# A channel mix on one Trainium2 core: two 64-row contractions in place of one block-diagonal contraction over 128 rows

## The chip, the cores and the metric

The kernel runs on one core of a Trainium2 chip. The metric is the device time of one execution in microseconds. Three runs of the kernel before gave 2972.39, 2974.68 and 2974.85 us; the median is 2974.68 us.

## The reference, cut to what matters

An input of 4 images with 64 channels of 256 x 256 goes through four layers. Layers 0, 1 and 3 are long convolutions: each channel is convolved causally with a separable 256 x 256 filter that a small network generates, and the input times a bias is added. Layer 2 is the one that the change touches. It takes a 2-D Haar transform of every channel, scales the coefficients, mixes the 64 channels at every coefficient with a 64 x 64 matrix, shrinks the result towards zero, does this with two sets of weights, adds the two, transforms back and adds the input:

```python
f1 = haar2d(x)
acc = jnp.zeros_like(f1[:, :conv_w.shape[1]])
for i in range(v.shape[0]):                       # 2 sets
    f3 = f1 * v[i]
    f4 = jnp.einsum('bchw,oc->bohw', f3, conv_w[i])   # 64 channels -> 64
    f5 = jnp.sign(f4) * jax.nn.relu(jnp.abs(f4) - tau[i])
    acc = acc + f5
y = haar2d(acc, inverse=True)
return y + x
```

The scale v[i] doesn't depend on the channel, so the kernel applies it after the mix.

## The kernel before

The kernel has one function, `conv_seq_kernel`, which writes its instructions in an order that it plans itself. Every piece of work is registered with `at(tick, place, run, unit)`; at the end the pieces are sorted by tick and place and run. A tick holds one step each of several pipelines, so that one image's mixing lies among the convolutions of the next image. The tile framework then adds the semaphores and may exchange neighbours on an engine[...].

For each image b there are three stages.

- `convolutions(b, ...)`: per channel, layers 0 and 1 (`first` and `second` twice, each with one `contract`, four TensorE instructions at L190 and L191), the Haar transform along the width on VectorE (`pairs`, `levels`: L257, L258, L269, L270), a split into two parts (`split`, L280 on ScalarE and L281 on VectorE), and along the height on TensorE (`down`, L288). The coefficients go to memory (`coef`).
- `mixing(b, start, n_act)`: 64 groups g, one per tick. `load` fetches a tile `f` of 128 partitions x 2 x 256: partitions 0 to 63 hold the 64 channels of one block of coefficient rows (k = 0), partitions 64 to 127 those of the other block (k = 1); a group has two rows q of each block. `mix` (L335) multiplies them by the weights on TensorE. The result `px` has the coefficient's column on the partitions and 1024 numbers per partition, two PSUM banks: for each half h of the columns, each row q, each block r, both weight sets i and the 64 outputs o. VectorE scales the first `16 - n_act` of the 16 pieces of 64 (L357), ScalarE the other `n_act` one by one (L359). `n_act` is 12 for images 0 to 2 and 6 for image 3. `shrink` takes the size and the sign on ScalarE (L365, L366) and subtracts the threshold on VectorE (L367); `signed` (L372) and `add` (L376) finish on VectorE. `add` writes into `z`, which holds all mixed coefficients of an image.
- `inverse(b, ...)`: per channel c, ScalarE gathers the channel out of `z` with a strided copy (L396), TensorE transforms along the width (L403, L404) and the height (L416), and VectorE joins the parts (L420, L423, L424). Layer 3 follows, at once or, for a third of the channels, put off to the mixing of the last image (`convolution`).

In `mix`, `wb` is a 128 x 256 matrix. Its upper 64 rows hold the weights of both sets in columns 0 to 127 and zeros in the rest; its lower 64 rows hold zeros and then the same weights. So one instruction with 128 rows and 256 columns does both blocks, and half of the products are with zero:

```python
for q in range(2):
    for h in range(2):
        nc.tensor.matmul(ps[:, h, q, :], f[:, q, h * P : (h + 1) * P],
                         wb.rearrange("p r n -> p (r n)"), start=True, stop=True)
```

`psx` has two buffers of two banks for `px`, `psm` four banks for all other products. Every fp32 product appears in the trace as two passes, each with a load of the stationary operand and a stream of the moving one; so the four instructions of a group are 8 matmul records and 8 load records.

Of the kernel before, what the change touches and what calls it, by code (L numbers as in the profile page):

```python
# [9 lines left out]
F32 = mybir.dt.float32  # L10
# [6 lines left out]
B, C, S, EMB, ORD = 4, 64, 256, 33, 64  # L17
P = 128
# [19 lines left out]
def conv_seq_kernel(ctx, tc, x, fz, fw, bias, decay, haar, haar_row, factors, vt, taut, wmix, out):  # L38
# [14 lines left out]
    nc = tc.nc  # L53

    const = ctx.enter_context(tc.tile_pool(name="const", bufs=1))
# [3 lines left out]
    zpool = ctx.enter_context(tc.tile_pool(name="zpool", bufs=1))  # L59
# [4 lines left out]
    psx = ctx.enter_context(tc.tile_pool(name="psx", bufs=2, space=PSUM))  # L64
# [4 lines left out]
    hbr = const.tile([P, P], F32R, name="hbr")  # L69
    hrow = const.tile([P, 2, P], F32, name="hrow")  # L70
    hsinv, ident = hrow[:, 0, :], hrow[:, 1, :]
    wb = const.tile([P, 2, P], F32, name="wb")
    bsb = const.tile([P, 3, C], F32, name="bsb")


    z = zpool.tile([P, 2, S, C], F32, name="z")

    sd = zpool.tile([P, 8, 2, 2, P], F32, name="sd")
    keep = [dram.tile([C, P, 2, 2, P], F32, name=f"keep{b}") for b in range(B)]
# [4 lines left out]

    room = z.rearrange("p h r c -> p (h r c)")
    free = [0]

    def part(n, parts=P):  # L90
        free[0] += n
        return room[:parts, free[0] - n : free[0]]
# [55 lines left out]
    def constants():  # L148
        signs = part(P)
        nc.sync.dma_start(hbt, haar[0])  # L150
        nc.sync.dma_start(signs, haar[1])
        nc.sync.dma_start(hrow, haar_row)
        nc.vector.memset(wb, 0.0)
        for r in range(2):
            nc.sync.dma_start(wb[r * C : (r + 1) * C, r, :], wmix)
        nc.scalar.copy(hb, signs)
        nc.scalar.copy(hbr, hbt)

# [19 lines left out]
    def toeplitz(layer, c, name):  # L178

        t = tp.tile([P, 2, S], F32, name=name, tag="toep")  # L180
        nc.sync.dma_start(t, ap(pads[layer], c * 2 * ROW, [[1, P], [ROW, 2], [1, S]]))
        return t
# [33 lines left out]

    def butterfly(b):

        d = mx.tile([P, 2, C], F32, name=f"bfly_{b}", tag="mag")
        nc.vector.tensor_sub(d, z[:, :, 0, :], z[:, :, 1, :])  # L220
        nc.vector.tensor_add(z[:, :, 0, :], z[:, :, 0, :], z[:, :, 1, :])
        nc.vector.tensor_copy(z[:, :, 1, :], d)

# [2 lines left out]
    def at(tick, place, run, unit):  # L228
        events.append((tick, place, len(events), run, unit))
# [86 lines left out]
    def mixing(b, start, n_act):  # L316

        st = {}

        def load(g):  # L320
            f = mx.tile([P, 2, S], F32, name=f"f_{b}_{g}", tag="f", bufs=3)
            nc.sync.dma_start(f, coef[b].rearrange("k c p w -> (k c) p w")[:, 2 * g : 2 * g + 2])
            st[g] = {"f": f}
            if g % GT == 0:
                t = mx.tile([P, 2, GT, 16], F32, name=f"vt_{b}_{g}", tag="vt")
                nc.sync.dma_start(t, scales[g // GT])
                st["vt", g // GT] = t

        def scale(g, i):
            return st["vt", g // GT][:, i, g % GT, :]  # L330

        def over(g, i, n):
            return scale(g, i)[:, :n].unsqueeze(2).to_broadcast([P, n, C])

        def mix(g):  # L335
            f = st[g]["f"]
            ps = psx.tile([P, 2, 2, S], F32, name=f"px_{b}_{g}", tag="mix")
            for q in range(2):
                for h in range(2):
                    nc.tensor.matmul(  # L340
                        ps[:, h, q, :],
                        f[:, q, h * P : (h + 1) * P],
                        wb.rearrange("p r n -> p (r n)"),
                        start=True,
                        stop=True,
                    )
            if g == 0:

                one, two = ps[:, :, 0, :P], ps[:, :, 0, P:]
                d = mx.tile([P, 2, P], F32, name=f"d_{b}", tag="mag")  # L350
                nc.vector.tensor_copy(d, two)
                nc.vector.tensor_sub(two, one, d)
                nc.vector.tensor_add(one, one, d)
            f4 = mx.tile([P, 16, C], F32, name=f"f4_{b}_{g}", tag="f4")
            px = ps.rearrange("p h q (r i o) -> p (h q r i) o", r=2, i=2)
            n = 16 - n_act
            nc.vector.tensor_tensor(f4[:, :n], px[:, :n], over(g, 0, n), ALU.mult)  # L357
            for j in range(n, 16):
                nc.scalar.mul(f4[:, j], px[:, j], scale(g, 0)[:, j : j + 1])  # L359
            st[g]["f4"] = f4  # L360

        def shrink(g):
            f4 = st[g]["f4"]
            mag = mx.tile([P, 16, C], F32, name=f"mag_{b}_{g}", tag="mag")
            nc.scalar.activation(mag, f4, AF.Abs)  # L365
            nc.scalar.activation(f4, f4, AF.Sign)  # L366
            nc.vector.tensor_sub(mag, mag, over(g, 1, 16))  # L367
            st[g]["mag"] = mag

        def signed(g):  # L370
            mag = st[g]["mag"]
            nc.vector.scalar_tensor_tensor(mag, mag, 0.0, st[g]["f4"], ALU.max, ALU.mult)  # L372

        def add(g):
            parts = st.pop(g)["mag"].rearrange("p (h r i) o -> p h r i o", h=2, i=2)
            nc.vector.tensor_add(z[:, :, 4 * g : 4 * g + 4, :], parts[:, :, :, 0, :], parts[:, :, :, 1, :])  # L376

        for g in range(S // 4):
            at(start + g - 2, 0, load, g)

            for s, (place, stage) in enumerate([(-2.5, mix), (-3.5, shrink), (-4.1, signed), (-4.2, add)]):
                at(start + g + s, place, stage, g)

    def inverse(b, start, put_off):

        st = {}

        def fetch(c):  # L390
            if c == 0:
                butterfly(b)
            r = mx.tile([P, 2, 2, P], F32, name=f"r_{b}_{c}", tag="f", bufs=3)
            nc.sync.dma_start(r, keep[b][c])
            a = mx.tile([P, 2, 2, P], F32, name=f"zc_{b}_{c}", tag="mag")
            nc.scalar.copy(a, z[:, :, :, c].rearrange("p h (i k) -> p h k i", k=2))  # L396
            st[c] = {"r": r, "z": a}

        def rows(c):
            a = st[c]["z"]  # L400
            ps = psm.tile([P, 2, 2, P], F32, name=f"pw_{b}_{c}", tag="mm")
            for m in range(2):
                nc.tensor.matmul(ps[:, m, 0, :], a[:, 0, m, :], hsinv, start=True, stop=True)  # L403
                nc.tensor.transpose(ps[:, m, 1, :], a[:, 1, m, :], ident)  # L404
            w = mx.tile([P, 2, 2, 2, P], F32R, name=f"w_{b}_{c}", tag="f4")
            nc.scalar.copy(w[:, 0], ps)  # L406
            nc.vector.tensor_tensor(w[:, 1], ps, w[:, 0].bitcast(F32), ALU.subtract)
            st[c]["w"] = w
            if c not in put_off:
                st[c][2] = toeplitz(2, c, f"t2_{b}_{c}")  # L410

        def cols(c):
            ps = psm.tile([P, 2, 2, P], F32, name=f"pu_{b}_{c}", tag="mm")
            flat = "p m e w -> p (m e w)"
            for i in range(2):
                nc.tensor.matmul(  # L416
                    ps.rearrange(flat), hb, st[c]["w"][:, i].rearrange(flat), start=(i == 0), stop=(i == 1)
                )
            t = io.tile([P, 2, 2, P], F32, name=f"t_{b}_{c}", tag="res", bufs=BUFS["res"])
            nc.vector.scalar_tensor_tensor(t, st[c]["r"], 0.5, ps, ALU.mult, ALU.add)  # L420
            u = io.tile([P, 2, S], F32, name=f"u_{b}_{c}", tag="y", bufs=BUFS["y"])
            v = u.rearrange("p m (w e) -> p m w e", e=2)
            nc.vector.tensor_add(v[:, :, :, 0], t[:, :, 0, :], t[:, :, 1, :])  # L423
            nc.vector.tensor_sub(v[:, :, :, 1], t[:, :, 0, :], t[:, :, 1, :])  # L424
            st[c]["u"] = u

        ends = last(b, st)
        for c in range(C):

            at(start + c, -1, fetch, c)  # L430
            at(start + c + 1, -9, rows, c)
            at(start + c + 2, -8, cols, c)
            if c in put_off:
                at(start + c + 3, -5, lambda c: nc.scalar.dma_start(late[b, c], st.pop(c)["u"]), c)
            else:
                for s, stage in enumerate(ends):
                    at(start + c + 3 + s, s - 7, stage, c)
# [28 lines left out]
    one, two, three = filters(0, nc.scalar), filters(1, nc.scalar), filters(2, nc.sync)  # L466
# [12 lines left out]
    for tick, do in enumerate([constants, None, None, *three[:-1], *tables()], 4):  # L479
        if do is not None:  # L480
            at(tick, 3, lambda unit, do=do: do(), 0)
# [4 lines left out]
    start = ready + 3  # L486
    for b in range(B):
# [10 lines left out]
        start = max(end + C, ready + 3)  # L498
# [112 lines left out]
```

## Time and profile before

The profiled execution took 2975.2 us and its span is 2973.4 us, so 1.8 us lie around the span; it stands 0.5 us above the median of the runs.

| | busy us | share of the span |
|---|---|---|
| PE (TensorE matmul) | 2913.8 | 98% |
| PEld (TensorE loads of the stationary operand) | 2615.1 | 88% |
| DVE (VectorE) | 2545.5 | 86% |
| ACT (ScalarE) | 2156.9 | 73% |
| L340 PE, the mix | 488.2 | 2048 records, mean 380 ns |
| L340 PEld, its loads | 369.5 | 2048 records, mean 190 ns |

A row of the groups reads: line, engine, operation, output<-inputs, shapes, number, then busy time, mean of one in ns, and the idle time just before with what ended it. Matmuls are pipelined: [...] neighbours overlap, and the spacing of the starts tells how fast they follow each other. In the timeline, "x8" means that eight instructions of a kind were merged into one row. The granted clock is full in all slices.

Mixing of image 0 lies at about 453 to 845 us, of image 1 at 1110 to 1515, of image 2 at 1780 to 2185 and of image 3 at 2440 to 2708. L340 is found nowhere else.

### The profile page before, as it was taken

To read this page: it belongs to the slowest core of one execution; us is meant where nothing else is said; L and a number is where in the kernel's file an instruction comes from. 1 tells how busy PE (TensorE), PEld (TensorE's weight loads), DVE (VectorE), ACT (ScalarE), POOL (GpSimd) and SP (SyncE) were. 2 spreads that over 40 slices of the span, in tenths; PEclk is the share of its full clock that TensorE was granted. 3 is DMA by queue.
4 is the path that set the end of the run, shared out by engine and by line. 5 is a ranking of instruction groups with operands and counts; after the bars stand their busy time and mean duration, and the time that the engine had idled before them with its cause. 6 is when DMAs were issued, how large, how long until landed. Compare 5 with 4: busy or idle time off the path is not lost. (4 is left out here: it accounts for less than half of the span.)

```text
span 2973.4 us, 52066 instructions
## 1 busy us (share of the span) xinstructions
PE 2913.8 (98%) x16950; PEld 2615.1 (88%) x16950; DVE 2545.5 (86%) x4571; ACT 2156.9 (73%) x5014; POOL 0.2 (0%) x4
## 2 busy tenths in 40 slices
PE   8999999999999999999999999999999999999999
PEld 6898988888888898888888988888888988888998
DVE  5766768999998879999989879999998889998776
ACT  2333338999986758889986668989986768887554
POOL 0000000000000000000000000000000000000000
PEclk9999999999999999999999999999999999999999
DMA  5877777666667876776777876777777878777676
GB/s 159 247 237 226 229 228 212 203 202 207 207 196 244 250 217 200 208 216 204 208 219 244 250 225 197 209 210 211 207 216 237 256 236 235 233 230 217 212 212 186
DMA packets 562497, 649.73 MB, mean 219 GB/s; under 512 B 44369, under 2 KB 447412, under 8 KB 562100
## 3 DMA queue, kind: packets, MB, share of 16 engines
q1 hardware_dynamic: 482996, 562.07, 64.8%
q10 hardware_dynamic: 79232, 84.34, 8.0%
q8 instruction: 137, 2.24, 0.3%
q14 instruction: 132, 1.08, 0.1%
HBM read 426.77 MB, written 219.48 MB: 217 GB/s over the span
## 5 line engine op out<-in xcount | busy, mean ns | idle before, releaser
L190 PE MATMUL py<-t,a 128*128 128x256 f32 x3072 | 919.0, 381 | 8.9 <-ACT a L199 5.5
L199 ACT COPY a<-pa 128x512 f32<-128x512 f32 x768 | 477.2, 621 | 387.9 <-PE pa L191 357.2
L359 ACT ACTIVATE f<-px,vt 128x64 f32<-128x64 f32 x2688 | 582.3, 358 | 143.5 <-DVE f L357 143.4
L191 PEld LDWEIGHTS py<-t,a 128*128 128x128 f32 x3072 | 583.4, 190 | 79.3
L191 PE MATMUL py<-t,a 128*128 128x128 f32 x3072 | 590.0, 274 | 0.0
L190 PEld LDWEIGHTS py<-t,a 128*128 128x128 f32 x3072 | 500.4, 191 | 50.9 <-ACT a L199 12.4
L340 PE MATMUL px<-wb,f 128*128 128x256 f32 x2048 | 488.2, 380 | 4.9 <-ACT f L359 4.9
L340 PEld LDWEIGHTS px<-wb,f 128*128 128x128 f32 x2048 | 369.5, 190 | 47.0 <-ACT f L359 6.7
L367 DVE TENSOR_TENSOR mag<-mag,vt 128x1024 f32<-128x1024 f32 x256 | 312.4, 1220 | 28.3 <-ACT mag L365 26.9
L190 PE MATMUL pa<-t,y 128*128 128x256 f32 x1024 | 311.6, 386 | 22.4 <-DVE y L212 20.3
L406 ACT CAST w<-pw 128x512 fp32r<-128x512 f32 x256 | 150.2, 587 | 227.0 <-PE pw L404 218.9
L372 DVE SCALAR_TENSOR_TENSOR mag<-mag,f 128x1024 f32<-128x1024 f32 x256 | 311.7, 1218 | 1.9
L190 PE MATMUL pa<-t,x 128*128 128x256 f32 x1024 | 305.9, 380 | 0.4 <-issue 0.4
L365 ACT ACTIVATE mag<-f 128x1024 f32<-128x1024 f32 x256 | 293.7, 1147 | 11.0 <-DVE z L376 8.8
L366 ACT ACTIVATE f<-f 128x1024 f32<-128x1024 f32 x256 | 285.2, 1114 | 3.0
L396 ACT COPY zc<-z 128x512 f32<-128x512 f32 x256 | 282.0, 1103 | 0.7 <-ACT w L406 0.4
L281 DVE TENSOR_TENSOR sp<-sd,sp 128x512 fp32r<-128x512 f32 x256 | 176.1, 688 | 91.4 <-ACT sp L280 90.2
L190 PE MATMUL pa<-t,u 128*128 128x256 f32 x772 | 232.8, 383 | 2.9 <-PE pu L416 1.6
L420 DVE SCALAR_TENSOR_TENSOR t<-r,pu 128x512 f32<-128x512 f32 x256 | 174.9, 683 | 60.4 <-PE pu L416 57.0
L212 DVE SCALAR_TENSOR_TENSOR y<-x,bsb,py 128x512 f32<-128x512 f32 x256 | 190.1, 742 | 37.9 <-PE py L191 36.1
L212 DVE SCALAR_TENSOR_TENSOR y<-y,bsb,py 128x512 f32<-128x512 f32 x256 | 190.0, 742 | 34.2 <-PE py L191 33.1
L191 PEld LDWEIGHTS pa<-t,x 128*128 128x128 f32 x1024 | 194.6, 190 | 26.3
(67 smaller groups left out, 4458.9 us busy)
## 6 DMA issues: line engine op xcount, KB each, us to landing
t<-pad SPq DMA_DIRECT2D x768, 256.0 KB, 3.9
x<-in_x SPq DMA_DIRECT2D x256, 256.0 KB, 3.6
keep<-sd SPq DMA_DIRECT2D x256, 256.0 KB, 2.9
coef<-co SPq DMA_DIRECT2D x256, 256.0 KB, 3.3
f<-coef SPq DMA_DIRECT2D x256, 256.0 KB, 3.2
r<-keep SPq DMA_DIRECT2D x256, 256.0 KB, 3.3
out_y<-y ACTq DMA_DIRECT2D x256, 256.0 KB, 3.6
late<-u ACTq DMA_DIRECT2D x63, 256.0 KB, 2.9
```

Of the source, the lines that this page charges most:

```text
L190: nc.tensor.matmul(ps[:, m, :], src[:, 0, m * P : (m + 1) * P], t[:, ::-1], start=True, stop=False)
L191: nc.tensor.matmul(ps[:, m, P:], src[:, 1, m * P : (m + 1) * P], t[:, : P - 1 : -1], start=False, stop=True)
L199: nc.scalar.copy(a, ps)
L212: nc.vector.scalar_tensor_tensor(y, s[res], bsb[:, layer, c : c + 1], ps, ALU.mult, ALU.add)
L281: nc.vector.tensor_tensor(w[:, 1], t, w[:, 0].bitcast(F32), ALU.subtract)
L340: nc.tensor.matmul(ps[:, h, q, :], f[:, q, h * P : (h + 1) * P], wb.rearrange("p r n -> p (r n)"), start=True, stop=True,)
L359: nc.scalar.mul(f4[:, j], px[:, j], scale(g, 0)[:, j : j + 1])
L365: nc.scalar.activation(mag, f4, AF.Abs)
L366: nc.scalar.activation(f4, f4, AF.Sign)
L367: nc.vector.tensor_sub(mag, mag, over(g, 1, 16))
L372: nc.vector.scalar_tensor_tensor(mag, mag, 0.0, st[g]["f4"], ALU.max, ALU.mult)
L396: nc.scalar.copy(a, z[:, :, :, c].rearrange("p h (i k) -> p h k i", k=2))
```

## The change

`wb` becomes a 128 x 128 matrix: the same weights of both sets, once in the upper and once in the lower 64 rows, with no zeros; the memset of the zeros goes. `mix` contracts each block's 64 channels by themselves: 8 instructions of 64 rows and 128 columns in place of 4 of 128 rows and 256 columns. The block r = 0 uses partitions 0 to 63, r = 1 uses 64 to 127, in turn. In the built program each of the 8 carries a tile of 64 x 128 of the array, at row 0 for r = 0 and at row 64 for r = 1; all other matmuls, save the two first products of a filter's network with 33 rows each, carry 128 x 128. All of block 0's results lie in one PSUM bank and all of block 1's in the other.

The order of the 16 pieces in `px` follows: block, half, row, set instead of half, row, block, set. So `z` gets the block as an outer dimension, `add`, `butterfly`, the gather at L396 and the tables that the host lays out (`coefficients`, `factors`) change their indices. The number of instructions, the elements of each and the transfers stay as they are. In the built programs TensorE's list is the same but for 8 rows in place of 4 per group; on the other engines' lists some neighbours change places.

```diff
-    wb = const.tile([P, 2, P], F32, name="wb")
+    wb = const.tile([P, P], F32, name="wb")
...
-    z = zpool.tile([P, 2, S, C], F32, name="z")
+    z = zpool.tile([P, 2, 2, P, C], F32, name="z")
...
-        nc.vector.memset(wb, 0.0)
         for r in range(2):
-            nc.sync.dma_start(wb[r * C : (r + 1) * C, r, :], wmix)
+            nc.sync.dma_start(wb[r * C : (r + 1) * C], wmix)
...
-            ps = psx.tile([P, 2, 2, S], F32, name=f"px_{b}_{g}", tag="mix")
-            for q in range(2):
-                for h in range(2):
-                    nc.tensor.matmul(
-                        ps[:, h, q, :],
-                        f[:, q, h * P : (h + 1) * P],
-                        wb.rearrange("p r n -> p (r n)"),
-                        start=True,
-                        stop=True,
-                    )
+            ps = psx.tile([P, 2, 2, 2, P], F32, name=f"px_{b}_{g}", tag="mix")
+            for h in range(2):
+                for q in range(2):
+                    for r in range(2):
+                        rows = slice(r * C, (r + 1) * C)
+                        nc.tensor.matmul(
+                            ps[:, r, h, q, :], f[rows, q, h * P : (h + 1) * P], wb[rows], start=True, stop=True
+                        )
...
-            px = ps.rearrange("p h q (r i o) -> p (h q r i) o", r=2, i=2)
+            px = ps.rearrange("p r h q (i o) -> p (r h q i) o", i=2)
...
-            parts = st.pop(g)["mag"].rearrange("p (h r i) o -> p h r i o", h=2, i=2)
-            nc.vector.tensor_add(z[:, :, 4 * g : 4 * g + 4, :], parts[:, :, :, 0, :], parts[:, :, :, 1, :])
+            parts = st.pop(g)["mag"].rearrange("p (s q i) o -> p s q i o", q=2, i=2)
+            rows = z.rearrange("p r h i c -> p (r h) i c")[:, :, 2 * g : 2 * g + 2, :]
+            nc.vector.tensor_add(rows, parts[:, :, :, 0, :], parts[:, :, :, 1, :])
...
-            nc.scalar.copy(a, z[:, :, :, c].rearrange("p h (i k) -> p h k i", k=2))
+            nc.scalar.copy(a, z[:, :, :, :, c].rearrange("p k h i -> p h k i"))
```

More of the change, by code (lines that the diff above doesn't have):

```diff
@@ L83, in conv_seq_kernel @@
     late = dram.tile([B, C, P, 2, S], F32, name="late")
-    room = z.rearrange("p h r c -> p (h r c)")
+    room = z.rearrange("p r h i c -> p (r h i c)")
     free = [0]
@@ L217, in butterfly @@
     def butterfly(b):
+        one, two = z[:, 0, :, 0, :], z[:, 1, :, 0, :]
         d = mx.tile([P, 2, C], F32, name=f"bfly_{b}", tag="mag")
-        nc.vector.tensor_sub(d, z[:, :, 0, :], z[:, :, 1, :])
-        nc.vector.tensor_add(z[:, :, 0, :], z[:, :, 0, :], z[:, :, 1, :])
-        nc.vector.tensor_copy(z[:, :, 1, :], d)
+        nc.vector.tensor_sub(d, one, two)
+        nc.vector.tensor_add(one, one, two)
+        nc.vector.tensor_copy(two, d)
     events = []
@@ L336, in mix @@
             f = st[g]["f"]
-            ps = psx.tile([P, 2, 2, S], F32, name=f"px_{b}_{g}", tag="mix")
-            for q in range(2):
-                for h in range(2):
-                    nc.tensor.matmul(
-                        ps[:, h, q, :],
-                        f[:, q, h * P : (h + 1) * P],
-                        wb.rearrange("p r n -> p (r n)"),
-                        start=True,
-                        stop=True,
-                    )
+            ps = psx.tile([P, 2, 2, 2, P], F32, name=f"px_{b}_{g}", tag="mix")
[6 more added lines that the diff above has]
+                        )
             if g == 0:
-                one, two = ps[:, :, 0, :P], ps[:, :, 0, P:]
+                one, two = ps[:, 0, :, 0, :], ps[:, 1, :, 0, :]
                 d = mx.tile([P, 2, P], F32, name=f"d_{b}", tag="mag")
@@ L570, in coefficients @@
         a = a.reshape(2, S, S)[:, down][:, :, along]
-        return lay(a.reshape(2, S // 4, 4, 2, P).transpose(4, 1, 3, 2, 0).reshape(P, S // 4, 16))
+        return lay(a.reshape(2, S // 4, 2, 2, 2, P).transpose(5, 1, 3, 4, 2, 0).reshape(P, S // 4, 16))
     local = _haar_local()
@@ L576 @@
     scaled = (half * np.float32(math.sqrt(0.5)))[level]
-    rows = np.repeat(np.abs(local).max(axis=1), 2).reshape(1, S // 4, 1, 4, 1)
+    rows = np.abs(local).max(axis=1).reshape(1, S // 4, 1, 1, 2, 1)
     signs = np.sign(local)
@@ L580 @@
         [
-            (rows**power * np.stack([first, np.full(P, second)], axis=1).reshape(P, 1, 2, 1, 1) * np.ones((1, 2))).reshape(
+            (rows**power * np.stack([first, np.full(P, second)], axis=1).reshape(P, 1, 1, 2, 1, 1) * np.ones((2, 1, 1, 2))).reshape(
                 P, S // 4, 16
```

## Prediction

> **What bounds the kernel now.** I read the share of busy time first, then the four stretches in which L340 runs, then the waits in them, then the timeline of one group. The page's first view:
>
> ```profile
> PE 2913.8 (98%) x16950; PEld 2615.1 (88%) x16950; DVE 2545.5 (86%) x4571; ACT 2156.9 (73%) x5014; POOL 0.2 (0%) x4
> ```
>
> TensorE is the first suspect, but the share is a mean over stages. The busy time by stretch, for the mixing of images 0, 1, 2 and 3 (columns: stretch, its length, then busy us with counts of PE, PEld, DVE, ACT, POOL, then clock, DMA share, GB/s):
>
> ```profile
> 453.00:830.00 377.00, 368.25 (x2020) 325.41 (x2019) 359.10 (x623) 346.71 (x993) 0.00 (x0) 1.00 0.68 205
> 1110.00:1510.00 400.00, 394.74 (x2206) 354.14 (x2205) 375.21 (x657) 355.20 (x1001) 0.00 (x0) 1.00 0.71 207
> 1780.00:2180.00 400.00, 394.82 (x2209) 354.35 (x2208) 372.64 (x652) 356.45 (x1003) 0.00 (x0) 1.00 0.71 207
> 2440.00:2715.00 275.00, 268.24 (x1447) 238.26 (x1445) 269.66 (x314) 238.76 (x569) 0.00 (x0) 1.00 0.79 233
> ```
>
> The reader is to see two things. PE is the bound where the mix runs (99% in the second and third stretch). And VectorE stands close behind: it leaves 17.9, 24.8, 27.4 and 5.3 us, together 75 us. In the last stretch it is busier than PE. Whatever TensorE saves, these stretches can't lose more than about 75 us.
>
> The waits between 1110 and 1510 us say what VectorE's 25 idle us are:
>
> ```profile
> DVE y L212 <- PE py L191: 10.7, 14, 1.2
> DVE mag L367 <- ACT mag L365: 6.8, 9, 1.3
> DVE sp L281 <- ACT sp L280: 2.6, 8, 0.8
> ```
>
> Less than half is waiting for TensorE; the rest waits for ScalarE, which is 89% busy there. The timeline of PE around one group:
>
> ```profile
> 1400.36 1.89 PE L340 MATMUL px<-wb,f 128*128 128x256 f32 x8
> 1402.09 0.38 PE L190 MATMUL py<-t,a 128*128 128x256 f32 x1
> ```
>
> The next work starts 1.73 us after the group's first pass: 8 passes of 0.216 us, with no gap. All 256 groups take 256 x 1.73 = 443 us of TensorE's time. That is what the change bears on.
>
> [...] L112, with 33 rows, and L340, with 128, both have loads of about 0.19 us (183 at the least, 190). So halving the rows makes no load and no pass shorter by itself; all gain must come from two tiles working at once.
>
> **The change part by part.** *Passes.* A group becomes 8 products of 128 columns, so 16 passes and 16 loads. The price of a 128-column pass is in the timeline of L403 and its loads:
>
> ```profile
> 1000.69 0.30 PEld L403 LDWEIGHTS pw<-hrow,zc 128*128 128x128 f32 x2
> 1000.91 0.14 PEld L404 LDWEIGHTS pw<-hrow,zc 128*128 128x128 f32 x1
> ...
> 1000.80 0.39 PE L403 MATMUL pw<-hrow,zc 128*128 128x128 f32 x2
> 1001.02 0.27 PE L404 MATMUL pw<-hrow,zc 128*128 128x128 f32 x1
> ```
>
> Two passes in 0.22 us: one per 0.11 us. Two loads of 0.19 us each end 0.30 us after the first began, so loads too follow each other at 0.11 us. In the 256-column passes of before, the loads had time to spare; with 128 columns load and stream are equally long. Two bounds follow. If the two row halves both load and stream side by side, the 16 passes take 8 x 0.11 = 0.88 us. If only one load can be under way at a time, streams side by side are worth nothing, since a pass needs its load: 16 x 0.11 = 1.76 us. Against 1.73 that is -0.85 or +0.03 us a group. [...] I take the first, and keep the second as the rival.
>
> *Mode switches.* Each group now switches from 128-row to 64-row tiles and back. The listing of the built program has 271 unbroken stretches of L340's successor (241 whole groups, 15 cut in two), so 542 switches. Before has one such switch amid running convolutions, where layer 3's 33-row product (a 64-row tile) comes between two contracts:
>
> ```profile
> 64.14 0.38 PE L191 MATMUL pa<-t,x 128*128 128x128 f32 x2
> 64.46 0.70 PE L112 MATMUL fp<-z 33*128 33x256 f32 x2
> 65.08 0.70 PE L190 MATMUL py<-t,a 128*128 128x256 f32 x2
> 65.62 0.27 PE L191 MATMUL py<-t,a 128*128 128x128 f32 x1
> ```
>
> From 64.14 to 65.62 us is 1.48 us. The passes are 2 of 0.11 and 4 of 0.214, together 1.08. So 0.40 us went into two switches, 0.20 each: the old stream ends, the loads of the new mode start only about 0.1 us later, and the first one isn't hidden. Both products also wait on semaphores, so 0.20 is an upper value if those waits bound; zero is the lower. I take 0.20: the two directions agree[...]. 542 x 0.20 = 108 us.
>
> *Sum on TensorE.* Parallel: 256 x (0.88 - 1.73) + 108 = -218 + 108 = -110 us, some 27 us per stretch. Serial: 256 x 0.03 + 108 = +116 us, 29 per stretch.
>
> *What of it reaches the end.* In the second and third stretch PE is the bound and 27 us would come off, but VectorE's room is 25 and 27 us, and some 10 us of that waits for ScalarE. I take 16 us each. In the first, the PE rows wait for VectorE (L212, 7.4 us) as often as the other way round, and the room is 18: I take 6. In the last, VectorE is 98% busy: 2. Together 40 us. Outside these stretches no L340 runs, and nothing changes.
>
> *Edits with one answer.* L376 writes four runs of 128 in place of two of 256; VectorE's rows for 512 elements take 685 (L376), 688 (L281), 689 (L269, 8-byte steps) and 683 ns (L420) whatever the pattern, so nothing is added or gained. The gather at L396 takes 1103 ns against 621 for L199's copy of as many elements from PSUM; the step in `z` goes from 512 to 256 bytes. It may stay or fall to about 620, 256 x 0.48 = 124 us of ScalarE at most; the inverse stages, where it runs, have ScalarE below 72% and PE at 100%, which hides it. If it grew by as much, ScalarE would stand near 90% there and still not bind. I take nothing. The memset at L153 (0.27 us, at 1.2 us) goes; two small loads of `wb` stay. L357 and L359 read as many elements from two banks as before; ScalarE's wait for L357 stays. No DMA moves past another except neighbours that change places; I take nothing, with 5 us to either side. No wait is added: the group still waits for `f` and a free `px`, and signals once, at its last product.
>
> Against the profiled execution: 2975.2 - 40 = 2935.2 us; the median stands 0.5 below, so **2935 us**.
>
> **The rivals.** *Serial loads (slower).* One mechanism: the load path takes one load at a time whatever the tile, so 16 loads at 0.11 us set the pace, and the switches are pure cost. For it: loads and passes are equally long at 128 columns, and the trace never shows two loads closer than 0.11 us. [...] Price: 29 us in each stretch. First: PE idles 9 us, take 20. Second and third: 28 each. Last: PE idles 7, take 22. Together +98 us: 3073. It decides once a pass of the group comes to over (1.73 - 0.42) / 16 = 0.082 us, between the 0.055 of the parallel and the 0.11 of the serial case.
>
> *Partly parallel.* Streams overlap but the issue of 32 records, or the order first tile twice and then the second, keeps them at 0.07 to 0.10 us a pass: 0.07 gives 256 x (1.12 - 1.73) + 108 = -48 us of PE, of which a third reaches the end, 2960; 0.10 gives +74, about 3035.
>
> *Switches for nothing.* If the 0.20 was the semaphores' and a switch is free, the parallel case saves 54 us a stretch on PE and VectorE becomes the bound everywhere: at most 75 us, 2900. The serial case without it is +8 us, 2980.
>
> **How the numbers follow.** A measurement of this kernel tells some 0.2% (6 us) from no change. Parallel with a switch of 0.20 or less: 0.49 (2900 to 2960, on its own 2935). Serial: 0.38, with switches 0.33 (3045 to 3100), without 0.05. Partly parallel: 0.13 (2955 to 3045), split between the signs. Faster: 0.49 of the first and 0.03 of the last make 0.52, less 0.02 that VectorE takes away: 0.50. Same: 0.07. Slower: 0.43. The range runs from VectorE's bound, 2900, to 3080, which takes in the centre of the serial case; above it lies about 0.15, below it 0.03.
>
> **What would show it.** Right: in the timeline a group of 16 records spans about 0.9 us plus a gap of 0.2 on either side, loads start in pairs closer than 0.11 us, VectorE's share in 1110 to 1510 rises to 97 or 98%, and its waits for L191 shrink. Serial: starts of the mix's matmuls lie 0.11 us apart throughout, and ticks grow by 0.4 us. Wrong in the switches: no gap of 0.2 us at a group's ends. If the gather at L396 or the add at L376 changes by over 0.1 us a piece, my "nothing" for them is wrong.

## The result and the profile after

The changed kernel takes 2993.12 us (median of 4 runs, 2991.24 to 2998.09) against 2974.76 us for the kernel before (4 runs, 2972.39 to 2977.92). The ratio is 1.0064, interval 1.0046 to 1.0081: slower by 18 us, where 40 us less was forecast. The profiled execution took 2998.09 us, its span is 2996.3 us. In the changed file the lines from L190 to L212 stand one lower (L189 is before's L190); L340 became L343, L357 L356, L359 L358, L365 and L367 L364 and L366; L376 and L396 stayed. From the first start of the mix to its last start, the four mixings of before run from 454 to 860, 1092 to 1533, 1766 to 2206 and 2436 to 2708 us, which is wider for images 0 to 2 than was said ahead of the prediction; those of after run from 453 to 864, 1096 to 1540, 1776 to 2222 and 2455 to 2730.

The busy time of the kernel after, on its page:

```profile
PE 2833.4 (95%) x18998; PEld 2512.1 (84%) x18998; DVE 2546.9 (85%) x4570; ACT 2159.9 (72%) x5014; POOL 0.2 (0%) x4
```

TensorE lost 80 us of busy time and the end came 23 us later. The same four stretches as before, each inside a mixing save the last, which begins 15 us ahead of it and ends 15 us short of its end (columns PE, PEld, DVE, ACT, POOL, clock, DMA share, GB/s):

```profile
453.00:830.00 377.00, 345.87 (x2455) 298.99 (x2453) 353.72 (x614) 344.05 (x984) 0.00 (x0) 0.99 0.67 202
1110.00:1510.00 400.00, 374.31 (x2651) 327.79 (x2651) 369.69 (x647) 353.52 (x995) 0.00 (x0) 1.00 0.69 205
1780.00:2180.00 400.00, 371.95 (x2627) 325.72 (x2626) 367.75 (x644) 348.57 (x986) 0.00 (x0) 1.00 0.69 204
2440.00:2715.00 275.00, 246.08 (x1943) 214.40 (x1942) 262.18 (x315) 228.23 (x536) 0.00 (x0) 0.98 0.79 231
```

Every engine is busy for less of the same time than before: in the second stretch PE 20 us, VectorE 5.5 us, ScalarE 1.7 us. So TensorE was relieved and no other engine filled up. And the granted clock, full in every slice of before, is 0.99 and 0.98 in two stretches.

The mix itself did what the prediction expected. The timeline of one group of the kernel after:

```profile
1402.87 0.39 PE L190 MATMUL pa<-t,y 128*128 128x128 f32 x2
...
1403.19 0.97 PEld L343 LDWEIGHTS px<-wb,f 64*128 64x128 f32 x16
1403.19 1.16 PE L343 MATMUL px<-wb,f 64*128 64x128 f32 x16
...
1404.28 0.30 PEld L189 LDWEIGHTS pa<-t,x 128*128 128x128 f32 x2
1404.28 0.70 PE L189 MATMUL pa<-t,x 128*128 128x256 f32 x2
```

The single records behind the x16 (starts in us, from the trace):

```
loads    1403.186 1403.193 | 1403.294 1403.301 | 1403.403 1403.410 | ...
matmuls  1403.188 1403.194 | 1403.401 1403.408 | 1403.513 1403.519 | ... | 1404.071 1404.078
```

The two row tiles start 6 or 7 ns apart, and a pair follows the last by 0.11 us (the second follows the first by 0.21). The last pass of the old mode began at 1402.983, 0.11 us after the one before it, so its stream is put to end at 1403.09; the first stream after the group is put behind its load, at 1404.386, where the next load starts. That is 1.30 us where before had 1.73: 0.43 us less, times 256 groups 110 us. It is no single case: 176 of the 237 groups that stand whole in the trace take, as this one does, 1.296 or 1.297 us from the last start of the old mode to the first recorded start after them.

The waits between 1110 and 1510 us, first of the kernel before (two rows that the prediction didn't show), then of the kernel after (waiting engine and line, what it waited for, us in all, times, longest):

```profile
ACT f L359 <- DVE f L357: 41.1, 42, 2.5
...
PEld pa L190 <- DVE y L212: 8.7, 12, 1.9
```

```profile
ACT f L358 <- DVE f L356: 45.2, 51, 3.4
PEld pa L189 <- DVE y L211: 24.0, 21, 2.1
PE pa L189 <- DVE y L211: 20.0, 20, 2.0
DVE sp L281 <- ACT sp L280: 13.8, 17, 1.1
DVE mag L366 <- ACT mag L364: 10.2, 10, 2.8
```

The first row was there to be read before. ScalarE was busy for 355.2 of those 400 us and waited 41.1 us for VectorE's scaling: 396 us together; for TensorE it waited 2.3 us (L199 <- L191). So it had next to no time that a faster TensorE could fill directly, though its busy share says 89%. VectorE's wait for TensorE (L212 <- L191, 10.7 us) has gone from the top of the list, TensorE's wait for VectorE rose from 8.7 to 24.0 us, and VectorE waits longer for ScalarE (2.6 to 13.8, 6.8 to 10.2).

The granted clock fell to half in four pieces, one in the first mixing and three in the last. Here are the windows just ahead of the four, and then two of the pieces:

```profile
558.90:562.30 3.40, 1.47 (x7) 0.71 (x5) 3.40 (x7) 0.43 (x1) 0.00 (x0) 1.00 0.19 74
2548.90:2552.30 3.40, 1.76 (x21) 1.42 (x19) 3.30 (x5) 3.40 (x9) 0.00 (x0) 1.00 0.91 287
2637.60:2641.00 3.40, 1.25 (x18) 0.97 (x16) 3.40 (x4) 2.99 (x7) 0.00 (x0) 1.00 0.78 233
2716.10:2719.50 3.40, 0.78 (x14) 0.59 (x13) 3.40 (x6) 2.99 (x9) 0.00 (x0) 1.00 0.79 240
```

```profile
562.30:569.13 6.83, 5.76 (x24) 4.86 (x25) 5.54 (x13) 6.43 (x20) 0.00 (x0) 0.50 0.55 151
...
2719.50:2722.91 3.41, 3.41 (x14) 2.77 (x12) 3.12 (x4) 2.44 (x4) 0.00 (x0) 0.50 0.33 117
```

Each piece at 0.50 follows 3.4 us in which PE was busy for 0.78 to 1.76 us, while VectorE was at work nearly throughout. The pieces make 20.5 us at half clock, so up to 10 us of TensorE's work is lost in them, an estimate: half of the 20.5.

### The profile page after: what moved, and what is told of

The parts are those of the page before. It is cut to its first block, busy times and chain, and to the rows that moved or that the text cites. A ratio compares the mean times of both kernels' runs of the same rounds, so it can differ in the third digit from the quotient of the medians.

```text
span 2996.3 us, 56145 instructions
## 1 busy us (share of the span) xinstructions
PE 2833.4 (95%) x18998; PEld 2512.1 (84%) x18998; DVE 2546.9 (85%) x4570; ACT 2159.9 (72%) x5014; POOL 0.2 (0%) x4
## 3 DMA queue, kind: packets, MB, share of 16 engines
q14 instruction: 132, 1.08, 0.1%
## 5 line engine op out<-in xcount | busy, mean ns | idle before, releaser
L189 PE MATMUL py<-t,a 128*128 128x256 f32 x3072 | 945.2, 389 | 48.8 <-ACT a L198 43.0
L358 ACT ACTIVATE f<-px,vt 128x64 f32<-128x64 f32 x2688 | 580.6, 348 | 162.4 <-DVE f L356 162.4
L190 PEld LDWEIGHTS py<-t,a 128*128 128x128 f32 x3072 | 585.2, 190 | 80.2
L190 PE MATMUL py<-t,a 128*128 128x128 f32 x3072 | 591.5, 274 | 0.0
L189 PEld LDWEIGHTS py<-t,a 128*128 128x128 f32 x3072 | 484.5, 191 | 108.1 <-ACT a L198 59.4
L189 PE MATMUL pa<-t,y 128*128 128x256 f32 x1024 | 316.4, 391 | 69.4 <-DVE y L211 69.3
L366 DVE TENSOR_TENSOR mag<-mag,vt 128x1024 f32<-128x1024 f32 x256 | 312.3, 1220 | 30.7 <-ACT mag L364 29.0
L343 PE MATMUL px<-wb,f 64*128 64x128 f32 x4096 | 307.1, 286 | 14.9 <-ACT f L358 14.9
L189 PE MATMUL pa<-t,x 128*128 128x256 f32 x1024 | 308.9, 383 | 1.6 <-issue 1.3
L364 ACT ACTIVATE mag<-f 128x1024 f32<-128x1024 f32 x256 | 292.6, 1143 | 13.6 <-DVE z L376 12.2
L343 PEld LDWEIGHTS px<-wb,f 64*128 64x128 f32 x4096 | 254.8, 188 | 50.6 <-ACT f L358 17.6
L396 ACT COPY zc<-z 128x512 f32<-128x512 f32 x256 | 282.4, 1104 | 9.0 <-DVE z L222 6.2
L365 ACT ACTIVATE f<-f 128x1024 f32<-128x1024 f32 x256 | 283.1, 1106 | 6.3 <-DVE y L211 2.3
L189 PE MATMUL pa<-t,u 128*128 128x256 f32 x772 | 232.8, 383 | 3.6 <-PE pu L416 2.3
L189 PEld LDWEIGHTS pa<-t,y 128*128 128x128 f32 x1024 | 156.4, 192 | 88.7 <-DVE y L211 86.1
L190 PEld LDWEIGHTS pa<-t,y 128*128 128x128 f32 x1024 | 195.1, 191 | 26.6
```

The costliest lines, as they stand in the source:

```text
L189: nc.tensor.matmul(ps[:, m, :], src[:, 0, m * P : (m + 1) * P], t[:, ::-1], start=True, stop=False)
L190: nc.tensor.matmul(ps[:, m, P:], src[:, 1, m * P : (m + 1) * P], t[:, : P - 1 : -1], start=False, stop=True)
L343: nc.tensor.matmul(ps[:, r, h, q, :], f[rows, q, h * P : (h + 1) * P], wb[rows], start=True, stop=True)
L396: nc.scalar.copy(a, z[:, :, :, :, c].rearrange("p k h i -> p h k i"))
```

## The experiments

Three causes were to be told apart: (a) the framework's new order of the instructions; (b) TensorE's saving is real, but the loop between ScalarE and VectorE sets the pace; (c) idling costs TensorE clock. "Mixing lengths" are the time from the first to the last matmul of the mix, in the profiled execution, for images 0 to 3. They are 406.5, 440.5, 440.3 and 271.3 us before and 411.1, 444.0, 445.7 and 275.4 after, so 17.5 of the 23 us lie in them.

**The order and the mix, each alone.** The two programs issue the same pieces, but the framework sorts them a little differently: 865 of 4570 places of VectorE's list, 388 of 5337 of ScalarE's, 145 of 10267 of TensorE's and 91 of 2194 of SP's hold another instruction (so TensorE's list isn't quite the same, as was said ahead of the prediction). Manual dependencies that set no semaphore hold one kernel's order in the other; in the traces the sequence of operations and tiles on VectorE and ScalarE is then the same in every place:

```diff
+    for engine, packed in lists.items():
...
+        for a, b in zip(order, order[1:]):
+            tc.add_manual_dep(own[b], own[a].name,
+                mybir.DependencyInfo(mybir.DependencyClass.NoSync, mybir.DependencyReason.DATA), reason="hold")
+    hold(ORDER)
```

The changed mix with before's order:

> The changed kernel, with the order of instructions on every engine held to that of the kernel before (its mix's 4 products stand as 8). Theory A (order): the framework's scheduler, given the new mix, exchanged neighbours on VectorE, ScalarE and the transfer queue, and those exchanges cost what was lost; with the old order the loss of 18 us goes and some of TensorE's saving shows: 2935 to 2970 us. Theory B (the other engines bound): VectorE and ScalarE pace the mixing whatever their exact order, and the row-tiled mix itself loses the 18 us: 2985 to 3000 us.

The old mix with after's order:

> The kernel before, with the order of instructions on every engine held to that of the changed kernel; the mix is the old block-diagonal one. Theory A (order): the new order is the worse one, so it is slower than before by about 18 us or more, since TensorE here has no saving to set against it: 2990 to 3030 us. Theory B: the order matters little, 2970 to 2982 us.

Measured: 2981.87 us for the first (ratio 1.0024, 1.0014 to 1.0033), 2983.92 for the second (1.0033, 1.0021 to 1.0046), 2974.3 before. Both lie between the two forecasts put down for them: neither cause is the whole. The order costs 9.6 us by itself and the changed mix 7.6 us, together 17 of the 18. Nothing of TensorE's 110 us reached the end with the changed mix. The mixing lengths say the same: 405.5, 441.8, 441.9 and 274.7 for the changed mix in the old order, with none of the 28 us per image gone from them. The stretches between the mixings, where no mix runs, grew too: by 5.5 us in the changed kernel, by 3.9 with the old mix in the new order and by 1.9 with the changed mix in the old one, so most of that goes with the order.

**The threshold left out.** If VectorE's work were the bound, 256 pieces of 1.22 us less would show. From here on each program has the order that the framework gives it, save in the two runs that fill TensorE up again.

```diff
             nc.scalar.activation(f4, f4, AF.Sign)
-            nc.vector.tensor_sub(mag, mag, over(g, 1, 16))
```

With the old mix:

> The kernel before without the subtraction of the threshold (L367 on VectorE is left out, so the shrinking is not done; 256 instructions of 1.22 us, 312 us of VectorE's time). TensorE is the bound of the mixing in the kernel before, so both theories expect little: 2950 to 2975 us.

With the changed mix:

> The changed kernel without the subtraction of the threshold (L366 on VectorE is left out, so the shrinking is not done). If TensorE's saving is real (0.33 us a group, some 84 us in all) and is only kept back by VectorE, it shows here against the old mix with the same part left out: 60 to 85 us less than that, about 2880 to 2900 us. If the saving is not real, or ScalarE alone holds it back, the two are within 20 us of each other.

Measured: 2977.1 us (ratio 1.0008, 1.0000 to 1.0017) and 2963.5 us (0.9961, 0.9947 to 0.9974). The stretch 1110 to 1510 us of the old mix without the threshold, and its first wait:

```profile
1110.00:1510.00 400.00, 392.46 (x2188) 351.65 (x2187) 315.97 (x594) 352.37 (x989) 0.00 (x0) 1.00 0.68 204
```

```profile
ACT f L359 <- DVE f L357: 46.0, 37, 2.5
```

VectorE came down from 375 to 316 us and the kernel was no faster. PE was busy for 98% there too, so this run alone doesn't tell TensorE from ScalarE as the bound. ScalarE's busy time and this one wait still make 398 of 400 us. With the changed mix the kernel is 13.6 us shorter than that, in the branch of the forecast for a saving that is not real or that ScalarE alone holds back (within 20 us), though TensorE had 110 us less to do. But the images differ. The mixing lengths are 405.2, 444.9, 447.1 and 265.7 with the old mix and 401.9, 445.0, 445.3 and 249.6 with the changed one. In images 1 and 2 nothing is gained over before with both TensorE and VectorE relieved: there VectorE's busy time was not the second bound, and what stayed is ScalarE and its wait. In image 3 the changed mix is 16 us shorter than the old one, which fills PE there. The stretch 2440 to 2690 us, old mix first:

```profile
2440.00:2690.00 250.00, 247.73 (x1359) 222.07 (x1358) 195.58 (x239) 218.55 (x519) 0.00 (x0) 1.00 0.81 239
```

```profile
2440.00:2690.00 250.00, 238.58 (x1952) 209.67 (x1951) 206.17 (x254) 234.14 (x558) 0.00 (x0) 1.00 0.83 255
```

So in the last image, where VectorE was 98% busy before, its own work did hold the saving back, as the prediction had it.

**The shrinking left out.** Size, sign, threshold and product are replaced by one copy on VectorE.

```diff
-            nc.scalar.activation(mag, f4, AF.Abs)
-            nc.scalar.activation(f4, f4, AF.Sign)
-            nc.vector.tensor_sub(mag, mag, over(g, 1, 16))
...
-            nc.vector.scalar_tensor_tensor(mag, mag, 0.0, st[g]["f4"], ALU.max, ALU.mult)
+            nc.vector.tensor_copy(mag, st[g]["f4"])
```

With the old mix:

> The kernel before with the shrinking left out (no size, no sign, no threshold, no product; VectorE copies the scaled mix in the product's place), which takes 2.2 us of ScalarE's and about 1.8 us of VectorE's time from each group. Its mixing can only be bound by TensorE then. If TensorE was the bound of the mixing already (my prediction's reading), little changes: 2950 to 2975 us. If VectorE and ScalarE set the pace, 20 to 60 us go: 2915 to 2955 us.

With the changed mix:

> The changed kernel with the same shrinking left out. The trace has a group at 1.30 to 1.40 us with its two switches against 1.73; with both other engines out of the way all of it should come off: 256 x 0.33 to 0.43 us, so 70 to 110 us less than the old mix with the same part left out. If instead row tiling costs TensorE something that the records hide, the two lie within 20 us.

Measured: 2942.18 us (ratio 0.9891, 0.9876 to 0.9906) and 2891.09 us (0.972, 0.9707 to 0.9733): the changed mix is 51 us shorter. The stretch 1110 to 1510 us of the two, old mix first:

```profile
1110.00:1510.00 400.00, 400.00 (x2254) 361.74 (x2253) 296.24 (x620) 254.64 (x909) 0.00 (x0) 1.00 0.73 213
```

```profile
1110.00:1510.00 400.00, 387.05 (x2797) 343.93 (x2796) 305.34 (x648) 259.84 (x931) 0.00 (x0) 1.00 0.73 218
```

In this stretch PE has no gap with the old mix, VectorE and ScalarE have 100 us or more of idle time each, and the saving appears: the mixing lengths fall from 401.1, 430.9, 430.8 and 262.9 to 396.1, 417.7, 420.7 and 242.5. This is the direct evidence that TensorE does get quicker. It is less than half of the 110 us, and short of the 70 to 110 that were expected. PE is at 97% with the changed mix, ScalarE waits 116.5 us for VectorE's scaling there, and 10 us ran at half clock; how the rest is split over these was not settled.

**Two tiles for the results.** ScalarE's wait for L357 was put down to both engines reading one tile. Here each bank is a tile of its own (r = 0 and 1 in the changed mix, the column halves in the old), and ScalarE begins with the pieces of the bank that VectorE doesn't read (8 in images 0 to 2):

```diff
-            ps = psx.tile([P, 2, 2, 2, P], F32, name=f"px_{b}_{g}", tag="mix")
+            ps = [psx.tile([P, 2, 2, P], F32, name=f"px{r}_{b}_{g}", tag=f"mix{r}") for r in range(2)]
...
-            for j in range(n, 16):
-                nc.scalar.mul(f4[:, j], px[:, j], scale(g, 0)[:, j : j + 1])
+            for j in [*range(max(n, 8), 16), *range(n, 8)]:
+                nc.scalar.mul(f4[:, j], px[j // 8][:, j % 8], scale(g, 0)[:, j : j + 1])
```

With the changed mix:

> The changed kernel with its product in two tiles of one bank each, and ScalarE taking the 8 pieces of the second bank first, so that it no longer waits for VectorE's read of the first bank before its first piece (in the last image VectorE reads 10 pieces, so it needs a second, small instruction there). Theory C: ScalarE's wait for VectorE's scaling (48 us of 400 between 1110 and 1510 us in the changed kernel) closes a loop of the two engines, which keeps the pace whatever TensorE does. Without the wait the loop opens and TensorE's saving shows: 2925 to 2965 us. If the pace is set by the sum of VectorE's own work, it stays at 2985 to 3000 us.

With the old mix:

> The kernel before with the same two tiles and the same order of the pieces. Theory C: the loop opens here too, but TensorE stands at 99% in the mixing and takes over at once: 2960 to 2975 us, 10 to 40 us slower than the changed mix with two tiles. If the pace is set by VectorE's own work: 2970 to 2985 us.

Measured: 2974.86 us (ratio 1.0003, 0.9994 to 1.0012) and 2971.1 us (0.9991, 0.9984 to 0.9997). The changed kernel won 18 us by it, the old one 3; the first is above the forecast of an open loop (2925 to 2965), and the changed mix is not yet the faster of the two. Its single runs lie wide apart, from 2966.77 to 2987.6 us. Between 1110 and 1500 us ScalarE's wait for VectorE's scaling fell from 44.4 to 24.2 us with the changed mix and from 39.4 to 1.2 with the old one, where a wait of 30.4 us for TensorE took its place. So the wait came from how the two engines shared the results; whether the one tile made it, or that ScalarE began with pieces of the bank that VectorE reads, was not separated, as the edit changes both. The mixing of images 1 and 2 now is quicker with the changed mix (431.0 and 429.7 against 434.0 and 436.2), but that of image 3 is slower (284.5 against 279.3, both longer than the 271.3 of before): there VectorE has ten pieces, which with two tiles take two instructions. So `n_act` of the last image went from 6 to 8:

```diff
-        mixing(b, start, 12 if b + 1 < B else 6)
+        mixing(b, start, 12 if b + 1 < B else 8)
```

With the changed mix:

> The changed kernel with two tiles, as in the run of two tiles before, and in the last image ScalarE takes 8 pieces in place of 6, so that VectorE reads exactly one bank in one instruction and neither engine waits for the other's bank. In the run before, the last mixing took 284 us against 275 because of VectorE's second instruction (64 of them). Theory C: that comes off again and more, about 20 us: 2945 to 2962 us, faster than both kernels. If ScalarE becomes the bound of the last mixing (2 more pieces of 0.2 us in each of 64 groups, 26 us, on 238 of 275): 2965 to 2980 us.

With the old mix:

> The kernel before with two tiles and 8 pieces for ScalarE in the last image. TensorE, at 99% in the second and third mixing, holds it there; the last mixing gains what the changed one gains, unless TensorE holds that too: 2955 to 2968 us, and 3 to 15 us slower than the changed mix in the same form.

Measured: 2961.97 us (ratio 0.9959, 0.9947 to 0.9972) and 2967.32 us (0.9977, 0.9967 to 0.9987). The first is 12 us shorter than the kernel before and is the best with the whole computation. The changed mix is 5 us better here, but that isn't the mixing's doing alone: in the profiled executions the four mixing lengths together differ by 1.2 us (408.5, 431.9, 431.5 and 270.5 against 405.9, 434.0, 436.4 and 267.4), while 4.1 us lie behind the last mixing, where no mix runs. The orders were not held in these four runs. In the best kernel 1653 of VectorE's 4570 places hold another instruction than in the changed kernel, more than the 865 that cost 9.6 us, so how much of the 18 us, and of the 12, is the order and how much the open loop was not separated. What the traces show is the wait itself. The waits between 1780 and 2180 us, old mix first:

```profile
ACT f L368 <- PE px L340: 30.7, 39, 1.1
...
ACT f L368 <- DVE f L361: 3.8, 8, 1.3
```

```profile
ACT f L366 <- DVE f L359: 28.1, 22, 2.6
PEld pa L189 <- DVE y L211: 23.5, 23, 1.9
...
ACT f L366 <- PE px L343: 2.7, 5, 0.5
```

With two tiles ScalarE waits 30.7 us for the old mix, and 2.7 for the changed one. So the faster mix takes away a wait that now counts, and most of that time becomes a wait for VectorE again. It gains 6.9 us in images 1 and 2, and images 0 and 3, where five of its six pieces at half clock lie, give 5.7 of it back.

**TensorE filled up again.** With before's order held, the changed mix issues the four products of the second half of the columns twice, to the same place:

```diff
-            for h in range(2):
+            for h in (0, 1, 1):
```

> The changed mix with the old order of instructions, and the four products of the second half issued twice, to the same place (the result is the same; 8 more passes a group, 0.44 us, 113 us of TensorE's time in all, about as much as the change saved). The run with the old order but without them took 2981.9 us, 7.6 above before, and had 17 us of half clock in four pieces. If TensorE's time in the mix is worth nothing and the half clock costs the rest: 2974 to 2980 us, with no half clock left. If TensorE's time counts, the 0.44 us show: 3010 us or more. If the rest is the two switches, which stay: about 2982 us.

Measured: 2975.61 us (ratio 1.0006, 1.0000 to 1.0013), beside 1.0024 without the filling: some 113 us more for TensorE (an estimate: 256 groups x 4 pairs of 0.11 us) made the kernel about 6 us faster. No piece runs at half clock any more, in place of 17 us, and the stretch 1110 to 1510 us is before's again:

```profile
1110.00:1510.00 400.00, 394.64 (x3116) 352.10 (x3115) 374.37 (x657) 356.69 (x1008) 0.00 (x0) 1.00 0.70 208
```

```profile
ACT f L358 <- DVE f L356: 41.7, 42, 2.8
```

The mixing of image 3, where the half clock had been, took 270.8 us in place of 274.7; those of images 0 to 2 stayed within 0.7 us. So with one tile TensorE's time in the mix is worth nothing either way, and where it idled more the kernel took 6 us longer. That it is the clock that costs, and not the shifted starts alone, is not shown; it rests on the two going together.

The same filling, for images 0 and 3, in the best kernel, with that kernel's order held:

```diff
-            for h in range(2):
+            for h in (0, 1, 1) if b in (0, B - 1) else (0, 1):
```

> The changed mix in two one-bank tiles, 8 pieces for ScalarE in the last image (2961.97 us), with the order of all instructions held as it was there, and in images 0 and 3 each group's four products of the second half of the columns issued twice, to the same place: 128 x 4 passes in pairs of 0.11 us, some 56 us of TensorE work that nobody needs. Theory (TensorE's saving is not on the path in these stretches, and its idling costs clock): the pieces of 3.41 us at half clock in images 0 and 3 (5 of 6) go, the granted clock is 1.000, and the time stays or falls by up to 8 us: 2954 to 2963. Rival (with the loop between ScalarE and VectorE opened, TensorE's time is on the path again): 56 us more on TensorE bring 10 to 40 us: 2972 to 3002.

Measured: 2980.05 us (ratio 1.001, 1.0003 to 1.0017), 18 us more than without, or 15.5 with each taken against the runs of the kernel before beside it. The theory that was put down for it fell, the rival held. Three pieces of 3.41 us at half clock were left in place of six, and yet the mixing lengths rose from 408.5 to 414.5 in image 0 and from 270.5 to 282.6 in image 3, and stayed in the others (431.8 and 430.2 after 431.9 and 431.5). The stretch 2440 to 2690 us, without and with the filling:

```profile
2440.00:2690.00 250.00, 239.66 (x1801) 211.71 (x1798) 244.57 (x290) 240.43 (x644) 0.00 (x0) 1.00 0.80 236
```

```profile
2440.00:2690.00 250.00, 250.00 (x2188) 225.31 (x2186) 235.53 (x276) 230.81 (x611) 0.00 (x0) 1.00 0.77 224
```

TensorE is the bound of that stretch once it is filled. So what a microsecond of TensorE is worth depends on the loop beside it: nothing with one tile, some 0.3 with two (15.5 to 18 us of an estimated 56, which is 128 groups x 4 pairs of 0.11). The filling also puts off each group's release by 0.44 us, by the same estimate; which of the two made the difference was not separated.

## Why the prediction was wrong

- *Passes.* Right. 0.11 us per pair of passes was forecast from L403 and L404 and measured; eight pairs take 0.89 us. That the two tiles would work at once was assumed, as no view of before shows it; in the trace of after the two loads of a pair start 6 or 7 ns apart, and so do its two matmuls. The rivals of serial loads (0.11 us a pass) and of a partial overlap (0.07 to 0.10) fell with it: a pass costs 0.055 us.
- *Mode switches.* Right. 0.88 + 2 x 0.20 = 1.28 us a group was forecast, 1.30 measured. The trace has 267 unbroken stretches in place of 271, which is 8 switches or 2 us less. So the rival of free switches fell too.
- *Sum on TensorE.* Right, 110 us by the time from group to group. Its busy time fell by only 80: passes at half clock take longer (in the piece from 562.30 us the mix's pairs follow each other by 0.21 us in place of 0.11), which is up to 10 us, and the rest is probably that the record of a pass reaches past its stream (0.27 us for 128 columns, with starts 0.11 us apart), which was not counted.
- *Edits with one answer.* L376 takes 685 ns and L396 1104 (before 685 and 1103), as forecast.
- *"What of it reaches the end."* This is the step that failed. It took PE for the bound "where the mix runs" and VectorE's 25 idle us for room, and so let 16 us come off in each of the middle stretches, 40 in all. With the order held, none came off, and 113 us of TensorE's time put back cost nothing. Two views contradicted the step before any run: ScalarE's busy time and its wait for L357 fill 396 of 400 us, and the prediction itself noted that less than half of VectorE's waiting was for TensorE, and that ScalarE's wait for L357 stays. It also read the first stretch wrongly: TensorE waited there for VectorE 13 times (7.4 us), VectorE for TensorE 6 times (2.6 us), not as often. A busy PE at 99% showed that TensorE was not waiting much, not that the others had time to spare. The runs without the threshold show that in images 1 and 2 VectorE's room was no room, those without the shrinking that the saving is real, those with two tiles that ScalarE's wait comes from sharing the results with VectorE. For the last stretch, with 2 us, the step was right in kind: VectorE's own work bound there.
- *"Neighbours that change places; I take nothing, with 5 us to either side."* Mis-sized: 9.6 us (6 to 14, from the interval), half of the loss. Which neighbours do it was not found. That outside the stretches of the mix nothing changes was off with it, by 5.5 us.
- *What the sum did not hold at all:* the half clock after stretches in which TensorE had less to do. The trace of after has four pieces of it, of 3.41 and 6.83 us, and in the 3.4 us ahead of each PE was busy for a quarter to a half of the time (0.78 to 1.76 us). The prediction counted this nowhere. With the old order some 6 us went with it, by the filled run.
- *What would show it.* VectorE's share was to rise to 97 or 98% in the second stretch and its waits for L191 to shrink. The waits did, but the share fell from 94 to 92%. That row tells "TensorE alone was the bound" from "it was one of three".

The time lies inside the range of 2900 to 3080 us, but on the other side from the forecast, and by none of the four cases it was built from.

## What to carry to other kernels

Before counting a saving on the busiest engine, add each other engine's busy time and its waits for engines other than that one. Where they fill the stretch, expect the saving to stay on the engine, as 110 us did here with the order held. Look for what makes that wait (here two engines that read one PSUM tile, in an order that begins in the same bank) and open it first: with two tiles and two more pieces on ScalarE the changed kernel went from 18 us slower to 12 us faster than before, and 6.5 of the 12 came with the old mix too. And when an edit changes tiles or indices, compare the built orders, since a reshuffle of neighbours alone cost 10 us of 2975.

## What the runs showed of the hardware

TensorE's clock fell with the engine far from idle. In the changed kernel, windows of 3.4 us with PE busy for 0.78, 1.25, 1.47 and 1.76 us were each followed by half clock. Of the windows of 3.41 us counted from the start of a piece, the lowest that was not followed by it was busy for 1.62 us (48%); at other offsets one of 1.14 us (33%, from 2683.56 us) was not. The kernel before has no half clock amid its work; counted from the start of its clock's record, its least busy window there, from 1206.34 us, had 1.86 us (55%). So in the changed kernel 48% went without half clock and 1.76 us, 52%, didn't: no sharp border shows. With two tiles and 8 pieces for ScalarE in the last image, a window busy for 2.30 of 3.40 us (68%) was followed by half clock. With the order of before held, adding useless products to the changed mix took the pieces away and shortened it by 6 us. A switch between 128-row and 64-row tiles cost 0.20 us each way: around a group of the changed kernel the two took 0.41 us (1.30 less 0.89 for its eight pairs), around a single product of the kernel before 0.40 (1.48 less 1.08 for its passes). So grouping the products of one mode is worth, by estimate, as much as two 128-column passes of 0.11 us per switch that it saves.
